# A 3x3 convolution by small tiles: shared products written into the columns' accumulators by ScalarE, and four products in five of six row combinations

## The chip, the core and the metric

The kernel runs on one core of a Trainium2 chip. Its time is the device time of one execution in microseconds (us). A core has five engines that run side by side and wait for one another through semaphores: TensorE (PE; its weight loads are listed as PEld) multiplies matrices into PSUM, an accumulator memory of eight banks; VectorE (DVE) and ScalarE (ACT) work element by element and can read and write PSUM and SBUF; GpSimd (POOL) works element by element on SBUF alone; SyncE (SP) issues DMA transfers. Each engine runs its own instructions in a fixed order.

## The reference

Two residual bottleneck layers, one after the other, in float32, on 64 images of 1024 channels and 14 x 14 pixels:

```python
out = relu(bn(conv(out_of_layer_before, w1, b1, 1, 0), g1, be1))   # 1x1, 1024 -> 256
out = relu(bn(conv(out, w2, b2, 1, 1), g2, be2))                   # 3x3, 256 -> 256
out = bn(conv(out, w3, b3, 1, 0), g3, be3)                         # 1x1, 256 -> 1024
out = relu(x + softplus(residual_scale)[0] * out)
```

`bn` takes the mean and variance of each channel over all images and pixels, so every convolution has to be complete before the next step can use its result.

## The kernel before

**The stages.** For each of the two layers: the first 1x1 convolution (in the first layer alone, in the second fused with the end of the first layer), the 3x3 convolution (`conv2`), a stage that gathers second moments for the last normalization (`gram`, `conv3_stats`), and the last 1x1 convolution with the residual. The 1x1 convolutions use a scheme with seven products for eight (`Seven`). The 3x3 convolution is the stage that the change touches, and two helpers beside it: `filters`, which transforms the 3x3 filters, and `norm`, which applies the normalization.

**How the 3x3 convolution is computed.** The rows of an image are taken four at a time. Six linear combinations of the input rows (i = 0 to 5) are each convolved along the line with a transformed filter, and the six results are combined into four output rows. Along a line, the columns are split into an odd and an even half (`WH` = 7 columns each). For a pair of output columns there are two ways. With *five products* a combination uses D1D2, applied to the sum of the two halves (one product that both columns share), and D1, D3 for the odd and D2, D0 for the even columns. With *four products* it uses SUM and DIFF, applied to the sum and to the difference of the halves (both shared), and D3M1 and D0M2 for one column each; the last two need a further array `v` of column differences. `FOUR` (line 67) lists the combinations with four products: 3, 4 and 5.

**Tiling.** Channels are 2 slots of 128 partitions (`MS`), for input (`s`) and output (`o`). Images go in 8 groups of 8. Combinations 0, 1, 2 and 5 have 4 rows of tiles, so a matmul has 4 x 8 x 7 = 224 columns; 3 and 4 have 3 rows, 168 columns. Each product is 4 matmuls (2 x 2 slots), so a combination is 20 matmuls with five products and 16 with four.

**Per pair of combinations.** `pairs` (line 492) runs over the groups and, in each, over the pairs (1, 2), (3, 4), (5, 0). `combine` makes the row combinations of a pair on VectorE (`r`), and in `ready` the sums of the halves on VectorE (line 531), the differences on GpSimd (line 534), `v` on VectorE (line 538) with its edges on ScalarE, and starts the load of the transformed filters `u` (line 547). `products` runs the matmuls of the pair. `finish` evacuates: ScalarE copies one shared product to SBUF (`ms`, lines 657 and 661); VectorE forms the half with the shared parts (`shared_part`, line 675) and adds the columns' own products (`column`, line 683). Then VectorE combines the results into output rows, which overwrite the input rows in `y`. The loop makes the combinations of the next pair before the products of the present one. For group 0 and the last group VectorE takes statistics (`stat`, line 693), for the others ScalarE does (`moment`, line 755).

**Order and buffers.** A scheduler of the language orders the instructions of each engine, except where the kernel fixes the order (`keep_in_program_order`). In `conv2` TensorE's matmuls are not fixed. All eight PSUM banks rotate under one tag, `ps`: a combination takes three or four in turn. Line 63 gives the numbers of SBUF buffers.

**Filters.** `filters` makes the transformed filters. For the first layer it runs on VectorE beside the first convolution. For the second layer it runs on GpSimd beside the moments stage (line 1101), in four pieces, with scratch tiles (`spare`) from the pool that holds the x tiles; the x tiles of the next stage (line 1121) reuse these buffers.

Of the kernel before, what the change touches and what calls it, by code (L numbers as in the profile page):

```python
# [33 lines left out]
FP = mybir.dt.float32  # L35
# [3 lines left out]
P = 128  # L39
# [23 lines left out]
BUFS = dict(u=3, t=3, r=4, sums=4, diffs=2, v=2, ms=3, f=2)  # L63
# [3 lines left out]
FOUR = 3, 4, 5  # L67
NKS = [4 if i in FOUR else 5 for i in range(NF)]
NK = max(NKS)
D0, D1D2, D3, D1, D2 = range(5)  # L70
D0M2, SUM, DIFF, D3M1 = range(4)
# [11 lines left out]
def bottlenecks(ctx: ExitStack, tc: tile.TileContext, x, w1s, w2s, w3s, pars, out):  # L83
# [73 lines left out]
    def filters(eng, b, s, o, spare):  # L157
# [24 lines left out]
        for i, (row, more, op, by) in parts.items():  # L182
# [7 lines left out]
            if i in FOUR:  # L190
                r0, r1, r2 = (row[:, k * P : (k + 1) * P] for k in range(3))
                ends = rest[:, w : w + P]
                eng.tensor_tensor(ends, r0, r2, ALU.add)
                eng.tensor_tensor(u[:, SUM], ends, r1, ALU.add)
                eng.tensor_tensor(u[:, DIFF], ends, r1, ALU.subtract)
                scaled(u[:, SUM : DIFF + 1], u[:, SUM : DIFF + 1], 0.5 * by)
                scaled(u[:, D0M2], r0, -by)
                scaled(u[:, D3M1], r2, by)
            else:
                scaled(u[:, 0:3, :].rearrange("p k m -> p (k m)"), row, by)  # L200
                eng.tensor_tensor(
                    u[:, D1 : D2 + 1], u[:, D0 : D3 + 1 : D3 - D0], u[:, D1D2 : D1D2 + 1].to_broadcast([P, 2, P]),
                    ALU.subtract,
                )
# [275 lines left out]
    def norm(s, y, aff):  # L480

        scale, shift = aff
        nc.scalar.activation(y, y, AF.Relu, bias=shift[:, s : s + 1], scale=scale[:, s : s + 1])
# [6 lines left out]
    def conv2(psum, pool, b, par, aff, stats):  # L490

        pairs = [(g, p) for g in range(NG) for p in ((1, 2), (3, 4), (NF - 1, 0))]
# [23 lines left out]
        def combine(g, pair, between=None):  # L516
# [4 lines left out]
            made = []  # L521

            def ready(i, r):
# [21 lines left out]
                u = pool.tile([P, MS * MS * NK * P], FP, tag="u", name="u", bufs=BUFS["u"])  # L545
                u = u[:, : MS * MS * NKS[i] * P].rearrange("p (s o k m) -> p s o k m", s=MS, o=MS, m=P)
                nc.sync.dma_start(out=u, in_=us[b][i])
                made.append((i, lines, r, sums, diffs, u))

            both = slice(0, MS)  # L550
            if pair[0] == 1:
# [11 lines left out]
                ready(1, ra)  # L563
                nc.vector.tensor_sub(rb, t1, t2)
                ready(2, rb)
            elif pair[0] == 3:
# [6 lines left out]
                ready(3, ra)  # L573
                stt(rb, t4, -2.0, t3)
                ready(4, rb)
            else:
# [7 lines left out]
                ready(NF - 1, rb)  # L584
                for s in range(MS):
                    stt(ra[:, s, 1:], rows(g, s, 0, 1, RT), 4.0, ra[:, s, 1:])
                ready(0, ra)
            return made

        def products(made, first):  # L590


            done = []
            for i, lines, r, sums, diffs, u in made:
                n = lines * WH
                four = i in FOUR

                def bank():
                    return psum.tile(2 * RT * GI * WH).rearrange("p (o n) -> p o n", o=MS)

                less = bank() if four else None
                m = bank()
                eos = [bank() for o in range(MS)]

                def shared(to, k, v, o, s):
                    nc.tensor.matmul(  # L606
                        to[:, o, :n], u[:, s, o, k], v[:, s].rearrange("p l c -> p (l c)"),
                        start=(s == 0), stop=(s == MS - 1),
                    )

                def columns(o, s, part):

                    odd, even = (eos[o][:, q, :n].rearrange("p (l c) -> p l c", c=WH) for q in range(2))
                    if four:
                        to, k, v = ((odd, D3M1, r[:, s, :, WH:]), (even, D0M2, r[:, s, :, :WH]))[part]
                        nc.tensor.matmul(to, u[:, s, o, k], v, start=(s == 0), stop=(s == MS - 1))  # L616
                        return
                    to, k, v = (
                        (odd, D1, r[:, s, :, WH:]),
                        (odd[:, :, : WH - 1], D3, r[:, s, :, WH + 1 :]),  # L620
                        (even, D2, r[:, s, :, :WH]),
                        (even[:, :, 1:], D0, r[:, s, :, : WH - 1]),
                    )[part]
                    start = s == 0 and part % 2 == 0
                    stop = s == MS - 1 and part % 2 == 1
                    if by_slot:

                        start, stop = s + part == 0, s == MS - 1 and part == 3
                    nc.tensor.matmul(to, u[:, s, o, k], v, start=start, stop=stop, skip_group_check=by_slot)  # L629

                by_slot = first and not done
                each = list(itertools.product(range(MS), range(MS)))
                if four:
                    for to, k, v in ((less, DIFF, diffs), (m, SUM, sums)):
                        for o, s in each:
                            shared(to, k, v, o, s)
                    for o in range(MS):
                        for part in range(2):
                            for s in range(MS):
                                columns(o, s, part)  # L640
                elif by_slot:
                    for s, o in each:
                        for part in range(4):
                            columns(o, s, part)
                    for o, s in each:
                        shared(m, D1D2, sums, o, s)
                else:
                    for o in range(MS):
                        for s in range(MS):
                            shared(m, D1D2, sums, o, s)  # L650
                        for part in range(4):
                            for s in range(MS):
                                columns(o, s, part)
                ms = pool.tile([P, MS, RT * GI * WH], FP, tag="ms", name="ms", bufs=BUFS["ms"])
                if i == 1:
                    for o in range(MS):
                        nc.scalar.activation(
                            ms[:, o, :n], m[:, o, :n], AF.Identity, bias=par[:, B2 + o : B2 + o + 1]
                        )
                else:  # L660
                    nc.scalar.activation(ms[:, :, :n], (less if four else m)[:, :, :n], AF.Copy)  # L661
                done.append((four, lines, m, ms, eos))
            return done

        def halves(f, lines):

            return f.rearrange("p o r (i q c) -> p o q (r i) c", i=GI, q=2)[:, :, :, :lines]

        def shared_part(item, f):

            four, lines, m, ms, eos = item
            if four:
                a, l = (v[:, :, : lines * WH].rearrange("p o (l c) -> p o l c", c=WH) for v in (m, ms))
                for q, op in enumerate((ALU.subtract, ALU.add)):
                    nc.vector.tensor_tensor(halves(f, lines)[:, :, q], a, l, op)

        def column(item, f, o):
            four, lines, m, ms, eos = item
            n = lines * WH
            to = more = halves(f, lines)[:, o]  # L680
            if not four:
                more = ms[:, o, None, :n].to_broadcast([P, 2, n]).rearrange("p q (l c) -> p q l c", c=WH)
            nc.vector.tensor_tensor(to, eos[o][:, :, :n].rearrange("p q (l c) -> p q l c", c=WH), more, ALU.add)

        def finish(g, pair, done, acc):

            fa, fb = (new("f", full if pair[0] == 3 else RT) for i in range(2))
            out_rows = [y_grp[:, :, g, k::4, :] for k in range(4)]
            to = {0: first_stats, NG - 1: stats[:, :, 1:]}.get(g)

            def stat(o, k, lines):
                if to is not None:
                    nc.vector.bn_stats(to[:, o, k, :], lines[:, o])

            if pair[0] in (1, 3):
                for item, f in zip(done, (fa, fb)):
                    shared_part(item, f)
                    for o in range(MS):
                        column(item, f, o)
            if pair[0] == 1:  # L700
                acc = new("fa"), new("fb")
                nc.vector.tensor_add(acc[0], fa, fb)
                nc.vector.tensor_sub(acc[1], fa, fb)
            elif pair[0] == 3:
                a, d = (v[:, :, :full] for v in acc)
                c, e = (new(tag, full) for tag in ("fc", "fd"))
                nc.vector.tensor_add(c, fa, fb)
                nc.vector.tensor_sub(e, fa, fb)
                for o in range(MS):
# [7 lines left out]
            else:  # L717
# [9 lines left out]
                for o in range(MS):  # L727
                    stat(o, 4, end)
# [441 lines left out]
```

## Time and profile before

Three runs: 2070.30, 2070.74 and 2072.93 us; the median is 2070.74. The profiled execution has a span of 2069.7 us at a granted TensorE clock of 0.987.

| engine | busy, us | share of the span |
|---|---|---|
| TensorE, matmuls | 2009.1 | 97% |
| TensorE, weight loads | 1709.2 | 83% |
| VectorE | 1572.0 | 76% |
| ScalarE | 809.3 | 39% |
| GpSimd | 657.5 | 32% |

The 3x3 convolution of the first layer lies between about 312 and 621 us, that of the second between about 1341 and 1647. The profile shows busy time for each engine, for the whole span or for a stretch of it, the chain of work that ended last, groups of equal instructions with their mean time and what they waited for, and the instructions in order of time. A line of the order of time gives start and length in us, the engine, the source line, the operation, what it writes and reads, and in brackets how long the engine was idle before it and what ended the idle time. A float32 matmul of the program shows as two records. Matmuls are pipelined, so the distance between two starts tells more of their cost than the length of one.

### The profile page before, as it was taken

How to read it: one execution, taken by the hardware profiler on the slowest of the kernel's cores; microseconds unless marked ns; L12 is line 12 of the kernel's file. 1: busy time of each engine (PE TensorE's matmuls, PEld its weight loads, DVE VectorE, ACT ScalarE, POOL GpSimd, SP SyncE). 2: the span in 40 equal slices, each digit the busy share in tenths (PEclk: the TensorE clock that was granted, in tenths of full speed). 3: DMA queues.
4: the chain of work that ended last, by engine and by line, in shares of the span. 5: the costliest groups of instructions: out<-in, count | busy, mean ns of one | idle time of the engine just before them, and what ended most of it. 6: DMA issues, size and time to landing. Idle time of an engine off the chain costs nothing.

```text
span 2069.7 us, 27894 instructions
## 1 busy us (share of the span) xinstructions
PE 2009.1 (97%) x10120; PEld 1709.2 (83%) x10120; DVE 1572.0 (76%) x2946; ACT 809.3 (39%) x1591; POOL 657.5 (32%) x668
## 2 busy tenths in 40 slices
PE   8999998999998989999999999899999899999998
PEld 4555558999998879999999999899999898555554
DVE  6776559999883466777777767699989734799997
ACT  1011116224225035555555555462332330555555
POOL 0100001122218953333343333210322000566665
PEclk9999999999999989999999999999999999999999
DMA  7664425555533244444444444255555420589998
GB/s 285 235 240 162 184 94 191 181 206 184 199 138 125 99 190 160 183 168 176 183 160 187 160 184 172 100 197 197 194 181 206 160 92 20 222 320 339 326 340 300
DMA packets 73338, 395.33 MB, mean 191 GB/s; under 512 B 7024, under 2 KB 38000, under 8 KB 44400
## 3 DMA queue, kind: packets, MB, share of 16 engines
q1 hardware_dynamic: 63168, 324.26, 43.6%
q10 hardware_dynamic: 5904, 51.91, 6.0%
q0 software_dynamic: 4128, 17.37, 2.2%
q8 instruction: 80, 1.31, 0.3%
q14 instruction: 58, 0.48, 0.1%
HBM read 276.60 MB, written 116.92 MB: 190 GB/s over the span
## 4 chain that ended last, share of the span: by engine, by line
PE 80%; DVE 6%; POOL 6%; DMA 4%; issue 3%; ACT 1%; SPq 0%; DVEq 0%; POOLq 0%; ACTq 0%
PE ay L155 13%; PE ps L629 13%; PE cy L155 13%; PE ps L606 9%; PE ap L155 7%; PE cp L155 7%; PE ps L616 6%; PE ax L155 4%; PE cx L155 4%; POOL spare L168 2%; PE cp L810 2%; DMA x<-mid 2%; DVE x L400 2%; PE ps L155 1%; PE ap L811 1%
## 5 line engine op out<-in xcount | busy, mean ns | idle before, releaser
L274 ACT ACTIVATE cu<-cy,scale 128x196 f32<-128x196 f32 (+1 forms) x552 | 257.0, 474 | 305.8 <-PE cy L155 297.4
L534 POOL TENSOR_TENSOR diffs<-r 128x336 f32<-128x336 f32 (+1 forms) x48 | 115.5, 2408 | 651.3 <-DVE r L514 453.9
L629 PE MATMUL ps<-r,u 128*128 128x224 f32 (+1 forms) x1536 | 293.7, 343 | 13.9 <-DVE r L562 7.0
L629 PEld LDWEIGHTS ps<-r,u 128*128 128x128 f32 x1536 | 279.3, 190 | 17.8 <-issue 14.8
L400 DVE SCALAR_TENSOR_TENSOR x<-cp,scale,x 128x196 f32<-128x196 f32 (+1 forms) x368 | 178.0, 484 | 84.4 <-PE cp L155 82.3
L274 ACT ACTIVATE x<-x,shift 128x392 f32<-128x392 f32 x368 | 211.7, 614 | 68.4 <-POOL x L426 52.1
L155 PE MATMUL cy<-ct,w3s 128*128 128x196 f32 (+1 forms) x736 | 222.3, 384 | 2.5 <-ACT cu L274 2.5
L421 POOL TENSOR_TENSOR x<-x,cu 128x196 f32<-128x196 f32 (+1 forms) x184 | 167.7, 912 | 175.6 <-ACT cu L274 167.8
L155 PE MATMUL ay<-at,w1s 128*128 128x196 f32 (+1 forms) x752 | 209.3, 381 | 1.0 <-ACT au L274 1.0
L426 POOL TENSOR_TENSOR x<-x,cu 128x392 f32<-128x392 f32 x124 | 125.9, 1015 | 193.3 <-DVE x L400 188.5
L155 PEld LDWEIGHTS ay<-at,w1s 128*128 128x128 f32 x752 | 136.5, 190 | 35.4 <-ACT au L274 1.9
L155 PEld LDWEIGHTS cy<-ct,w3s 128*128 128x128 f32 x736 | 134.2, 191 | 36.8 <-ACT cu L274 4.0
L606 PE MATMUL ps<-sums,u 128*128 128x224 f32 (+1 forms) x768 | 156.0, 337 | 0.0
L447 POOL TENSOR_TENSOR x<-x,cu 128x392 f32<-128x392 f32 x120 | 125.1, 1042 | 83.4 <-DVE x L400 78.4
L274 ACT ACTIVATE au<-ay 128x196 f32<-128x196 f32 (+1 forms) x141 | 53.7, 381 | 241.7 <-PE ay L155 235.8
L661 ACT ACTIVATE ms<-ps 128x448 f32<-128x448 f32 (+1 forms) x80 | 40.4, 504 | 266.8 <-PE ps L606 266.8
L606 PEld LDWEIGHTS ps<-sums,u 128*128 128x128 f32 x768 | 133.0, 189 | 0.1
L400 DVE SCALAR_TENSOR_TENSOR x<-cx,scale,x 128x196 f32<-128x196 f32 (+1 forms) x184 | 89.1, 484 | 57.0 <-PE cx L155 51.3
L155 PE MATMUL cy<-y,w 128*128 128x196 f32 (+1 forms) x416 | 130.4, 401 | 1.1 <-DVE x L891 1.1
L616 PE MATMUL ps<-v,u 128*128 128x168 f32 (+1 forms) x768 | 131.1, 322 | 0.0
L155 PE MATMUL cx<-y,w 128*128 128x196 f32 (+1 forms) x404 | 125.9, 397 | 0.6 <-DVE x L891 0.6
L616 PEld LDWEIGHTS ps<-v,u 128*128 128x128 f32 x768 | 123.8, 188 | 0.8
(209 smaller groups left out, 4080.3 us busy)
## 6 DMA issues: line engine op xcount, KB each, us to landing
x<-in_x SPq DMA_DIRECT2D x62, 1568.0 KB, 6.6
u<-u SPq DMA_DIRECT2D x48, 1280.0 KB, 5.5
x<-mid SPq DMA_DIRECT2D x32, 1568.0 KB, 9.3
u<-u SPq DMA_DIRECT2D x48, 1024.0 KB, 4.8
mid<-x ACTq DMA_DIRECT2D x31, 1568.0 KB, 5.1
out<-x SPq DMA_DIRECT2D x124, 392.0 KB, 6.6
u<-y POOLq DMA_DIRECT2D x12, 320.0 KB, 5.7
u<-spare POOLq DMA_DIRECT2D x12, 320.0 KB, 2.5
```

The lines of the kernel that those rows point to most:

```text
L155: tc.keep_in_program_order(nc.tensor.matmul(*args, **kw))
L168: eng.tensor_scalar(to, v, by, None, ALU.mult)
L274: tc.keep_in_program_order(nc.scalar.activation(*args, **kw))
L400: nc.vector.scalar_tensor_tensor(v, bank, self.scale[:, o : o + 1], v, ALU.mult, ALU.add)
L421: nc.gpsimd.tensor_add(self.part(1, 1), self.part(1, 1), u3)
L426: nc.gpsimd.tensor_add(v, v, self.u12)
L447: nc.gpsimd.tensor_add(v, v, self.u12[:, i * self.n : (i + 1) * self.n])
L534: nc.gpsimd.tensor_sub(diffs, r[:, :, :, :WH], r[:, :, :, WH:])
L606: nc.tensor.matmul(to[:, o, :n], u[:, s, o, k], v[:, s].rearrange("p l c -> p (l c)"), start=(s == 0), stop=(s == MS - 1),)
L616: nc.tensor.matmul(to, u[:, s, o, k], v, start=(s == 0), stop=(s == MS - 1))
L629: nc.tensor.matmul(to, u[:, s, o, k], v, start=start, stop=stop, skip_group_check=by_slot)
L810: nc.tensor.matmul(g0, zt[:, c, 0:P], zt[:, c, :], start=first, stop=last)
```

## The change

**Four products in more combinations.** `FOUR` becomes 0, 2, 3, 4, 5; only combination 1 keeps five products. This saves four matmuls each for combinations 0 and 2. `filters` makes the four-product filters for these two as well.

**Shared products go into the columns' banks.** A combination now has one bank for both output slots of its odd columns and one for the even columns. TensorE first runs the product that goes to both (DIFF with four products, D1D2 with five) into a bank of its own, `l` or `m`. ScalarE copies it, for DIFF with the sign of the half, into the odd and the even bank. TensorE then accumulates the columns' own products on top (`start=False`). With four products the SUM product still goes to SBUF (`ms`), and VectorE adds it while it evacuates (`add`). With five products nothing is left to add, and VectorE reads the two banks when it joins combination 1 with combination 2 into `fa` and `fb`. Four matmuls with the identity open the column banks once per layer.

**The order.** Work goes by single combinations, in the order 1, 2, 3, 4, 5, 0, in three steps: `start` (the first shared product and ScalarE's writes), `middle` (SUM and `ms`) and `columns`. TensorE's order is now fixed: start of the next combination, then middle and columns of the present one. The banks have four tags with two buffers each (`l`, `m`, `odd`, `even`). Norms and moments on ScalarE are spread over the combinations (`long_work`) and kept in order. The load of `u` is split into `ua` (the first shared filter) and `ub` (the rest).

```diff
-BUFS = dict(u=3, t=3, r=4, sums=4, diffs=2, v=2, ms=3, f=2)
+BUFS = dict(ua=4, ub=3, t=2, r=4, sums=4, diffs=3, v=3, ms=3, f=2)
-FOUR = 3, 4, 5
+FOUR = 0, 2, 3, 4, 5
...
+        for tag in COLUMNS * 2:
+            n = MS * RT * GI * WH
+            matmul(psum.tile(n, tag), ident, ident[:, :1].to_broadcast([P, n]), start=True, stop=True)
...
+            def start(self):
+                if self.first:
+                    self.columns()
+                    return
+                v = self.whole("l", DIFF, self.diffs) if self.four else self.whole("m", D1D2, self.sums)
+                self.banks = [self.bank(tag) for tag in COLUMNS]
+                if self.four:
+                    for bank, sign in zip(self.banks, (-1.0, 1.0)):
+                        nc.scalar.activation(bank, v, AF.Copy, scale=sign)
                 else:
+                    self.biased(self.banks, v)
+            def middle(self):
+                self.ms = None
+                if self.four or self.first:
+                    m = self.whole("m", SUM if self.four else D1D2, self.sums)
...
+                    self.biased([self.ms], m)
...
+            def add(self, f):
+                for q in range(2):
+                    nc.vector.tensor_tensor(
+                        half(f, q), self.column(q), self.column(q, self.ms), ALU.add
+                    )
...
+                fa = None if ca.ms is None else outputs(ca)
+                fb = outputs((yield))
+                a, d = new("fa"), new("fb")
+                if fa is not None:
+                    nc.vector.tensor_add(a, fa, fb)
+                    nc.vector.tensor_sub(d, fa, fb)
+                else:
+                    for q in range(2):
+                        nc.vector.tensor_tensor(half(a, q), ca.column(q), half(fb, q), ALU.add)
+                        nc.vector.tensor_tensor(half(d, q), ca.column(q), half(fb, q), ALU.subtract)
...
+        for k in range(NG * NF):
+            queue.extend(itertools.islice(made, 1))
+            for item in queue[1:2]:
+                item.start()
+            item = queue.pop(0)
+            item.middle()
+            if not item.first:
+                item.columns()
+            finished.send(item)
+            long_work(*divmod(k, NF))
...
-            conv2(Psum(scope, ["ps"], ps=8), pool, b, pb, aff, stats2)
+            conv2(Psum(scope, ["l"], l=2, m=2, odd=2, even=2), pool, b, pb, aff, stats2)
```

## The prediction

> **What bounds the kernel now.** I read the page first: TensorE is busy for 97% of the span and holds 80% of the chain that ended last. Then I went to the stage that changes, the 3x3 convolution, with a table of busy time over two stretches of 37 us, each one image group long, and over the stage behind it.
>
> ```profile
> core 0: us, PE busy (x) PEld busy (x) DVE busy (x) ACT busy (x) POOL busy (x), PEclk, DMA share, GB/s
> 421.00:458.00 37.00, 37.00 (x218) 36.78 (x217) 35.34 (x64) 12.12 (x25) 9.08 (x3) 1.00 0.55 192
> 458.00:495.00 37.00, 37.00 (x218) 36.78 (x217) 34.33 (x61) 12.11 (x25) 9.08 (x3) 1.00 0.54 192
> 640.00:740.00 100.00, 96.72 (x603) 84.15 (x603) 50.66 (x91) 13.39 (x14) 95.39 (x135) 0.98 0.25 91
> ```
>
> In the convolution TensorE never pauses, but VectorE has only 2.7 us of every 37 left. In 640 to 740 us GpSimd is busy for 95 of 100 us: it transforms the second layer's filters. The order of time shows what that leads to:
>
> ```profile
> 743.83 0.60 POOL L205 DMA_DIRECT2D u<-spare  x1 [0.30 <-POOL spare L168]
> 743.20 9.14 SPq L118 DMA_DIRECT2D x<-in_x  x3
> 751.41 0.42 DVE L400 SCALAR_TENSOR_TENSOR x<-cx,scale,x 128x196 f32<-128x196 f32 x1 [5.59 <-DMA x<-in_x]
> 752.22 1.02 PE L155 MATMUL cp<-y,w3s 128*128 128x196 f32 x2 [6.01 <-DVE x L400]
> ```
>
> The x tiles that the next stage needs reuse the filters' scratch tiles. Their load starts when GpSimd ends, and TensorE stands still for 6.01 us. So GpSimd's filter chain, 629 to 744 us, lies on the path today.
>
> TensorE's own pieces, from its order of time in one group:
>
> ```profile
> 457.68 1.67 PE L606 MATMUL ps<-diffs,u 128*128 128x224 f32 x8
> 463.77 0.92 PE L606 MATMUL ps<-sums,u 128*128 128x224 f32 x4
> 470.99 0.92 PE L606 MATMUL ps<-sums,u 128*128 128x224 f32 x4
> 485.45 1.30 PE L606 MATMUL ps<-diffs,u 128*128 128x168 f32 x8
> 490.05 1.30 PE L606 MATMUL ps<-diffs,u 128*128 128x168 f32 x8
> ```
>
> Starts apart: combination 5 (four products, 16 matmuls of 224 columns) takes 6.09 us, a five-product combination (20 matmuls) 7.22, combinations 3 and 4 (16 of 168 columns) 4.60 each. A group is 6.09 + 3 x 7.22 + 2 x 4.60 = 36.95 us; combination 5 starts 36.97 us apart from group to group.
>
> GpSimd beside VectorE, both in the convolution:
>
> ```profile
> 460.22 5.39 POOL L534 TENSOR_TENSOR diffs<-r 128x336 f32<-128x336 f32 x1 [8.89 <-DVE r L514]
> 464.75 1.14 DVE L675 TENSOR_TENSOR f<-ps,ms 128x448 f32<-128x448 f32 x2
> 398.19 0.93 POOL L534 TENSOR_TENSOR diffs<-r 128x336 f32<-128x336 f32 x1 [19.67 <-DVE r L514]
> 487.19 2.06 DVE L702 TENSOR_TENSOR fa<-f 128x896 f32<-128x896 f32 x1
> ```
>
> The same difference of 336 elements takes 0.93 us or 5.39. In the second case it ends only once VectorE reaches an operation that reads PSUM (464.75). The other way round, the addition of 896 elements takes 2.06 us beside a GpSimd difference instead of the usual 1.08.
>
> **What the Trainium skill says.** "SBUF — State Buffer", section "Who interferes with whom": a VectorE instruction with two SBUF inputs contends with a GpSimd instruction that reads SBUF, and one of them blocks fully. The lines above agree (5.39 against 0.93 us; 2.06 against 1.08). "PSUM — Partial Sum Buffer", "The four PSUM rules": writes of ScalarE leave a bank's written-bits alone, and a matmul without the start flag adds where they are set. That is why the change opens every column bank once with an identity matmul; no run here shows it yet. "ScalarE: Activation LUTs", "What ACT_TABLE_LOAD costs": an activation with immediates takes 186 ns + 0.833 ns per element, 559 ns for 448; the trace has 543 (L661).
>
> **The change part by part.** *TensorE.* Combinations 0 and 2 go from five products to four: 2 x (7.22 - 6.09) = 2.26 us less per group. TensorE alone would take 34.7. Over 16 groups that is the 36 us that the change is for. The four identity matmuls per layer (448 columns, about 0.75 us each by 392 columns in 0.66) fall into the 7 us for which TensorE waits at the start of the stage; I price them at nothing.
>
> *ScalarE.* Bank writes are 6 of 448, 4 of 336 and 4 of 224 elements per group, at 0.54, 0.45 and 0.43 us. With the moments and norms that it has already, it stays under 25 us of 37, so it is no bound, though it runs in order.
>
> *VectorE.* I count the built kernel's instructions for one group and price them by the distance between starts back to back: 0.53 us for 448 elements, 0.42 for 336, 0.77 for 672, 1.00 for 896, 0.86 for 768, 0.67 for 576, 0.30 for 224. Before: 16, 28, 8, 4, 1, 2, 1, which is 32.9 us. After: 14, 22, 9, 3, 3, 2, 1, which is 30.8. Before really took 34.33, so contention with three GpSimd operations costs 1.4. After has five such operations (differences for 0 and 2 too): 1.4 x 5/3 = 2.3, at least 1.4. VectorE needs about 33 us.
>
> *The new wait, and the one that I think decides.* Each kind of column bank has two buffers, taken in turn by combinations 1, 2, 3, 4, 5, 0. Combination 1's banks are read only together with the finished result of 2 (fa and fb), and 3 needs the same banks next. So ScalarE cannot write 3's even bank, and TensorE cannot run 3's even columns, before VectorE is through; behind them in TensorE's fixed order stand the first products of 5 and all of 4, and VectorE's next step waits for 4. One turn of this loop: VectorE from its read of 4's odd bank to the last reader of 1's even bank in the next group is all its work but four instructions (three of 336, one of 768), 30.8 - 2.1 = 28.7, plus 0.3 of waiting for 4's even bank; ScalarE 0.45 and two hand-overs of 0.1; TensorE 1.15 (even columns of 3) + 1.52 (first products of 5) + 1.15 + 1.15 (sums and odd columns of 4) = 4.97. Sum 34.6, plus contention of 1.4 to 2.3: 36.0 to 36.9. I take 2.3, since the two added GpSimd operations run beside the same stream of two-input additions, and call it 37.0: the same pace as today. Seven periods in each of two layers: 0.
>
> *Group 0.* Its statistics are VectorE work inside that loop: bn_stats and aggregates take about 4.3 us (1.73 for four, 0.91 for two, 0.44 for two, 0.6 twice, 0.28 twice). Today eight rotating banks let TensorE run on; the loop cannot. +4.3 per layer. Start and end differ by about +1: the first products of 5 come some 1 us earlier in group 0, since part of 4 now stands behind them, and that part comes back at the end. Together 2 x 5.4 = 10.8.
>
> *Filters of the second layer, on GpSimd.* A five-product filter costs a scaling of 384 and a subtraction of 256: 1.17 + 0.73 = 1.90 us. A four-product one costs 0.46 + 0.52 + 0.53 + 0.85 + 2 x 0.58 = 3.52. Two filters, four pieces: 8 x 1.62 = 13.0, less some 0.05 of overlap for each added instruction: 12. Nothing hides it: TensorE already waits at the end of this chain. +12. The first layer's filters run on VectorE, which is busy 108 of 181 us there: nothing. The loads of u, cut in two, carry fewer bytes and are ordered several combinations ahead: nothing.
>
> Sum: 2070.7 + 0 + 10.8 + 12 = 2093.5, say 2094.
>
> **The rivals.** *TensorE stays the bound (13%).* If GpSimd's operations fall beside VectorE's PSUM reads, contention vanishes and a group takes 34.7: 14 x -2.27 = -32, +2, +12: 2053. For it: VectorE's sum of 30.8 alone fits. Against it: 5.39 us in the lines above. *GpSimd is starved (27%).* The difference for 2 is asked for in a stretch of VectorE work without any PSUM read (from r of 2 to the read of 0's odd bank, 4 us). If it waits as at 460.22, TensorE's first products of 2 wait too: TensorE from these to 4's odd columns 21.4, VectorE from there to the read of 0's odd bank 14.8, GpSimd 1.17, hand-overs 0.2: 37.5 per group, +7 in all: 2101. *Both waits add up (7%).* The difference for 4 is late as well, 38.5 per group: +21 over my forecast, 2115. *The filter chain is hidden (5%).* 2082; it would need TensorE to be later than GpSimd there, against the 6.01 us.
>
> **How the numbers follow.** My forecast has 48%. The range leaves out the first rival and the one of both waits, 20% together: 2068 to 2110; contention at its lower bound (36.0 per group, -13) gives 2081, inside. Faster by over 0.2% is the first rival, 0.13; the space between it and the forecast gives 0.09 for within 0.2%; slower 0.78.
>
> **What would show it.** Right: combination 5 starts about 37 us apart from group to group, TensorE has gaps of 2 us or so per group, at the even columns of 3 or at the first products of 2; GpSimd's filter chain is 12 us longer and TensorE waits about 18 us at its end. Wrong: groups 34.7 us apart with TensorE at 37 of 37 busy, GpSimd differences all near 1 us, or a filter chain that no longer ends last. The weakest number is the contention, 1.4 to 2.3 us.

## The result and the profile after

The changed kernel takes 2106.5 us (median; 2103.7 to 2109.1), the kernel before 2071.8 beside it: 1.0165 times as long, 95% interval 1.0147 to 1.0184. The profiled execution has a span of 2105.4 us, 35.7 more than before. Cut at the same events in both traces (a 3x3 convolution ends here with GpSimd's first instruction after it), these come from:

| stretch | after minus before, us | forecast |
|---|---|---|
| start to the last matmuls of the first layer's first convolution | +2.8 | 0 |
| 3x3 convolution, first layer | +12.2 | +5.4 |
| filters of the second layer, to the load of x | +12.3 | +12 |
| end of the first layer, first convolution of the second | -1.5 | 0 |
| 3x3 convolution, second layer | +10.5 | +5.4 |
| the rest | -0.6 | 0 |

Two of the three large terms are in the 3x3 convolution, so look there first. The table of busy time over one period in the second layer (columns: length, then busy us of TensorE, its weight loads, VectorE, ScalarE, GpSimd, then the clock granted to TensorE):

```profile
1490.08:1527.84 37.76, 35.17 (x200) 34.28 (x201) 33.93 (x55) 21.54 (x43) 10.63 (x5) 1.00 0.52 174
```

Before, TensorE was busy for 37.0 of 37. Now a group takes 37.76 us and TensorE is busy for only 35.2. It has lost the matmuls it was to lose, and the period did not follow. The order of time on TensorE says where the pause is:

```profile
1490.08 1.75 PE L157 MATMUL m<-sums,ua 128*128 128x224 f32 x8 [2.38 <-issue]
...
1496.62 1.78 PE L157 MATMUL l<-diffs,ua 128*128 128x224 f32 x8 [0.21 <-POOL diffs L542]
...
1511.93 1.32 PE L157 MATMUL odd<-v,ub 128*128 128x168 f32 x8
1513.10 1.31 PE L157 MATMUL even<-v,ub 128*128 128x168 f32 x8
...
1516.90 1.32 PE L157 MATMUL odd<-v,ub 128*128 128x168 f32 x8
...
1523.77 1.69 PE L157 MATMUL even<-v,ub 128*128 128x224 f32 x8
1527.84 1.75 PE L157 MATMUL m<-sums,ua 128*128 128x224 f32 x8 [2.38 <-issue]
```

The even columns of combination 3 (1513.10), where the forecast put the wait, follow without a gap. TensorE pauses 2.38 us before `m<-sums,ua`, the first products of combination 1. "issue" means that the profile names no releaser; the operand does. These products read the sums of r for 1, and VectorE's order of time shows when those come:

```profile
1518.32 0.51 DVE L693 TENSOR_TENSOR f<-odd,ms 128x336 f32<-128x336 f32 x1 [2.32 <-ACT ms L636]
...
1525.59 1.08 DVE L578 TENSOR_TENSOR r<-t 128x896 f32<-128x896 f32 x1
1526.59 0.62 DVE L693 TENSOR_TENSOR f<-odd,ms 128x448 f32<-128x448 f32 x1
1527.13 0.61 DVE L539 TENSOR_TENSOR sums<-r 128x448 f32<-128x448 f32 x1
```

VectorE waits for combination 4 (1518.32; the profile names `ms`, which ScalarE had ready at 1517.55, but the odd columns of 4 end last, at 1518.22). Then it does the output arithmetic of the pair (3, 4), with one short wait of 0.34 us, and only then the sums of 1, which end at 1527.74; TensorE starts at 1527.84. That closes a loop: TensorE from the first products of 1 to the odd columns of 4, 1490.08 to 1518.22 = 28.14 us; hand-over 0.10; VectorE from 1518.32 to 1527.74 = 9.42; hand-over 0.10. The sum is 37.76, the period. In the list of waits TensorE stands 18.3 us at this place in each layer. That is about what eight groups were to save, 8 x 2.26 = 18.1.

The chain of filters on GpSimd ends like this now (against 743.20 and 6.01 us before):

```profile
769.52 1.84 POOL L170 TENSOR_SCALAR spare<-spare 128x128 f32<-128x128 f32 x3
770.52 9.07 SPq L120 DMA_DIRECT2D x<-in_x  x3
...
778.33 0.42 DVE L403 SCALAR_TENSOR_TENSOR x<-cx,scale,x 128x196 f32<-128x196 f32 x1 [13.73 <-DMA x<-in_x]
...
779.14 1.02 PE L157 MATMUL cp<-y,w3s 128*128 128x196 f32 x2 [15.04 <-DVE x L403]
```

TensorE waits 15.04 us at its end, 9.0 more than before.

### The profile page after: what moved, and what is told of

The parts are those of the page before. It is cut to its first block, busy times and chain, and to the rows that moved or that the text cites. A ratio compares the mean times of both kernels' runs of the same rounds, so it can differ in the third digit from the quotient of the medians.

```text
span 2105.4 us, 27919 instructions
## 1 busy us (share of the span) xinstructions
PE 1996.8 (95%) x9880; PEld 1682.0 (80%) x9880; DVE 1565.9 (74%) x2892; ACT 909.9 (43%) x1843; POOL 710.7 (34%) x736
## 4 chain that ended last, share of the span: by engine, by line
PE 71%; DVE 10%; POOL 8%; DMA 6%; issue 3%; ACT 1%; SPq 0%; DVEq 0%; POOLq 0%; ACTq 0%
PE ay L157 14%; PE cy L157 12%; PE ap L157 7%; PE cp L157 6%; PE odd L157 5%; PE even L157 5%; PE m L157 5%; PE l L157 5%; PE ax L157 4%; PE cx L157 3%; POOL spare L170 2%; PE cp L864 2%; POOL diffs L542 2%; DMA x<-mid 2%; DVE x L403 2%
## 5 line engine op out<-in xcount | busy, mean ns | idle before, releaser
L542 POOL TENSOR_TENSOR diffs<-r 128x448 f32<-128x448 f32 (+1 forms) x80 | 157.1, 1972 | 623.4 <-DVE r L580 302.7
L157 PE MATMUL cp<-y,w3s 128*128 128x196 f32 (+1 forms) x368 | 114.2, 392 | 17.7 <-DVE x L403 16.3
L157 PE MATMUL m<-sums,ub 128*128 128x224 f32 (+1 forms) x640 | 126.2, 341 | 0.0
L157 PE MATMUL l<-diffs,ua 128*128 128x224 f32 (+1 forms) x640 | 123.0, 335 | 1.9 <-POOL diffs L542 1.9
L864 PE MATMUL cp<-zt 128*128 128x257 f32 x392 | 120.7, 390 | 4.2 <-DVE zt L884 4.2
L157 PE MATMUL odd<-v,ub 128*128 128x224 f32 (+1 forms) x640 | 123.6, 334 | 0.0
L157 PE MATMUL even<-v,ub 128*128 128x224 f32 (+1 forms) x640 | 123.3, 334 | 0.0
L157 PEld LDWEIGHTS m<-sums,ub 128*128 128x128 f32 x640 | 114.5, 196 | 1.0
```

The source lines that it names most:

```text
L157: tc.keep_in_program_order(nc.tensor.matmul(*args, **kw))
L542: nc.gpsimd.tensor_sub(diffs, r[:, :, :, :WH], r[:, :, :, WH:])
L864: nc.tensor.matmul(g0, zt[:, c, 0:P], zt[:, c, :], start=first, stop=last)
```

## The experiments

**The theories.** A: the late sums for combination 1 set the period. B: GpSimd's starved difference for combination 2 does. C: both loops are as good as equally long, and only removing both helps. F: the loop of the forecast, in which combination 3 waits for the banks of 1. For B and C speak these lines of the changed kernel:

```profile
1491.68 4.88 POOL L542 TENSOR_TENSOR diffs<-r 128x448 f32<-128x448 f32 x1 [20.02 <-DVE r L580]
...
1497.42 0.93 POOL L542 TENSOR_TENSOR diffs<-r 128x336 f32<-128x336 f32 x1 [0.86 <-DVE r L524]
```

The difference for 2 takes 4.88 us, another one 0.93, as the rival "GpSimd is starved" had it; it ends at 1496.56, and TensorE starts on it at 1496.62 after waiting 0.21 us.

**Combination 1 started later.** Its first products go behind the columns of 0 in TensorE's order:

```diff
-            for item in queue[1:2]:
-                item.start()
+            ahead = queue[1:2]
+            for item in ahead:
+                if item.i != 1:
+                    item.start()
             item = queue.pop(0)
             item.middle()
             if not item.first:
                 item.columns()
+            for other in ahead:
+                if other.i == 1:
+                    other.start()
```

> The changed kernel, with the first products of combination 1 started only after the columns of combination 0, about 4 us later in TensorE's order; every instruction stays. In the changed kernel a group takes 37.76 us, and TensorE pauses 2.38 us before combination 1, for sums that VectorE makes late. Theory A (the late sums alone set the pace): the pause goes and nothing takes its place at once; a group takes 35 to 36 us, the whole 2072 to 2085. Theory C (two loops are tied: the second runs from TensorE's first products of 2 to the odd columns of 4, 21.6 us, over VectorE to r of 2, 11.1, and over GpSimd's starved difference, 4.9): the pause moves to the first products of 2, a group still takes about 37.5, the whole 2101 to 2107. Theory B (the starved GpSimd alone): as C. Theory F (my forecast, the banks of 1 and 3): no change, 37.76.

Measured: 2076.4 us (ratio to the kernel before 1.0025, 1.0015 to 1.0034), 30 us less than the changed kernel. A group takes 36.22 us, a little more than the 35 to 36 of theory A. The pause before 1 is gone, and one of 1.3 us stands before the products of 2:

```profile
1506.97 1.78 PE L157 MATMUL l<-diffs,ua 128*128 128x224 f32 x8 [1.28 <-POOL diffs L542]
```

So A is right about what bound the kernel, and the whole time lies in its band, but not that nothing takes its place. C is wrong as it was put: its second loop does set the pace now, but a shorter one, because the starved difference shrinks to 3.36 us when the two streams fall against each other differently (21.6 + 11.1 + 3.4 = 36.1):

```profile
1503.55 3.36 POOL L542 TENSOR_TENSOR diffs<-r 128x448 f32<-128x448 f32 x1 [18.48 <-DVE r L580]
```

**The difference for 2 on VectorE.**

```diff
-                    nc.gpsimd.tensor_sub(diffs, r[:, :, :, :WH], r[:, :, :, WH:])
+                    eng = nc.vector if i == 2 else nc.gpsimd
+                    eng.tensor_sub(diffs, r[:, :, :, :WH], r[:, :, :, WH:])
```

> The changed kernel, with the difference for combination 2 alone made by VectorE (about 0.53 us) instead of GpSimd (4.9 us, most of it starved). Theory B (the starved difference sets the pace): a group falls from 37.76 to 35 to 36 us, the whole to 2072 to 2085. Theory A and theory C (the late sums for combination 1 hold TensorE as long as the difference does): the pause of about 2.4 us before combination 1 stays, a group takes 37.2 to 38.2, the whole 2098 to 2112. Theory F (banks): VectorE has 0.5 us more to do in the loop, 38.2 us per group, 2112.

Measured: 2099.1 us (1.0136, 1.0117 to 1.0155), 7 us less than the changed kernel; 37.28 us per group, and the pause stays where it was:

```profile
1525.57 1.68 PE L157 MATMUL l<-diffs,ua 128*128 128x224 f32 x8
...
1556.68 1.75 PE L157 MATMUL m<-sums,ua 128*128 128x224 f32 x8 [2.38 <-issue]
```

B is out: the starvation is real and does not set the pace by itself. The 0.48 us per group that this edit gains are on TensorE: VectorE's part of the loop is 9.42 us as before (1547.16 to 1556.58), TensorE's 27.66 instead of 28.14, and the difference is the wait of 0.21 us in front of the products of 2, which is gone (1525.57). That wait lay inside the loop of A and, from start to start, cost 0.48.

**Both edits.**

> Both edits together: combination 1 starts after the columns of 0, and VectorE makes the difference for 2. Theory C (two tied loops): only now does the group get shorter, to 35 to 36 us, for TensorE's own work is 34.7 and VectorE's about 34.4; the whole 2070 to 2085. Theory A: the same as with the late start alone; theory B: the same as with the difference on VectorE alone. Theory F: no gain, 38 us per group.

Measured: 2065.7 us (0.9973, 0.9966 to 0.9981), 40.8 us less than the changed kernel, 5.5 less than the kernel before, and 4 under the lower end of theory C. One period:

```profile
1464.51:1499.77 35.26, 35.12 (x202) 34.38 (x200) 33.64 (x56) 21.33 (x43) 6.32 (x4) 1.00 0.57 187
```

TensorE is busy for 35.12 of 35.26 us: it is nearly the bound again. The parts alone gave 30 and 7, together 41, so the second edit is worth 11 us once the first is in. Busy time hides a rest: TensorE's own pieces need 34.7 us from start to start, and 0.4 of the other 0.6 lie at the even columns of 3. They start 1.46 us after its odd ones (1481.42), against 1.17 in the changed kernel, and right behind ScalarE's write of their bank, which had waited for VectorE's read of 2's:

```profile
1482.39 0.43 ACT L648 ACTIVATE even<-l 128x336 f32<-128x336 f32 x1 [1.19 <-DVE f L694]
1482.88 1.42 PE L157 MATMUL even<-v,ub 128*128 128x168 f32 x8
```

So a wait for column banks is there after all, milder than the forecast's and for the banks of 2 instead of those of 1. No run here separates what it is worth.

**One filter piece on VectorE.** Of the four pieces of the second layer's filters, the first is made by VectorE beside the moments stage, in two halves:

```diff
                     def piece(s, o):
...
+                        if (s, o) == (0, 0):
+                            return filters(nc.vector, 1, s, o, spare)
                         for _ in filters(nc.gpsimd, 1, s, o, spare):
                             pass
...
+                        beside[2] = lambda: (quarter.append(piece(0, 0)), next(quarter[0]))
+                        beside[8] = lambda: next(quarter[0], None)
```

> The changed kernel, with one of the four pieces of the second layer's filters made by VectorE (in two halves, their stores from SyncE's queue), the other three by GpSimd as before. If GpSimd's filter chain is on the path and costs the 12 us, as the forecast has it: the chain gets about 32 us shorter, the 15.0 us for which TensorE waits at its end shrink to nearly nothing (some wait for the x load remains), and the whole falls by 10 to 16 us, to 2091 to 2097. If the chain was hidden by something else that ends as late (the affine constants or the x load itself): a fall of under 3 us.

Measured: 2094.1 us (1.0109, 1.0092 to 1.0127), 12.4 us less than the changed kernel. The load of x starts at 739.19 instead of 770.52, and the wait of 15 us in front of `cp<-y,w3s` has gone:

```profile
739.19 12.30 SPq L120 DMA_DIRECT2D x<-in_x  x3
...
766.00 0.60 PE L157 MATMUL cp<-y,w3s 128*128 128x196 f32 x2 [0.33 <-DVE x L404]
```

The chain was on the path, as the forecast said. The gain stops near the length of the wait, though the chain ends 31 us earlier.

**The forecast's banks, made real.** In the changed kernel combination 3 gets the banks of 2 (lines in the next section). Here combinations 1, 3, 5 are tied to one pair and 2, 4, 0 to the other:

```diff
-                self.banks = [self.bank(tag) for tag in COLUMNS]
+                self.banks = [self.bank(tag + str((1, 2, 3, 4, 5, 0).index(self.i) % 2)) for tag in COLUMNS]
...
-            conv2(Psum(scope, ["l"], l=2, m=2, odd=2, even=2), pool, b, pb, aff, stats2)
+            conv2(Psum(scope, ["l"], l=2, m=2, odd0=1, odd1=1, even0=1, even1=1), pool, b, pb, aff, stats2)
```

> The changed kernel with the column banks tied to the turn that the forecast assumed: combinations 1, 3, 5 share one pair of banks, 2, 4, 0 the other, each named by hand, so that 3 must wait for the banks of 1. Nothing else is changed. Forecast's theory (banks in turn are what sets the pace): no difference, 37.8 us per group, no gap moves. Theory A (late sums set the pace, and the changed kernel's allocator gives 3 the banks of 2, which come free earlier): a gap appears in TensorE at the even columns of 3; if the forecast's loop is 36 to 37 us, it fits beside the 37.76 and the whole grows by under 5 us; if it is longer than that, by 7 times 2 times the difference.

Measured: 2133.3 us (1.0300, 1.0285 to 1.0315), 27 us more than the changed kernel. A wait now exists where the forecast put it, at the even columns of 3, and the old one is still there:

```profile
1526.39 1.68 ACT L277 ACTIVATE y<-y,shift,scale 128x1568 f32<-128x1568 f32 x1
1527.97 0.44 ACT L647 ACTIVATE even<-l 128x336 f32<-128x336 f32 x1
...
1528.46 1.42 PE L157 MATMUL even<-v,ub 128*128 128x168 f32 x8 [1.30 <-ACT even L647]
1543.32 3.33 PE L157 MATMUL m<-sums,ua 128*128 128x224 f32 x8 [2.38 <-issue]
```

F fell, and so did the "under 5 us" that I gave theory A if the new loop were no longer than the old. The new wait lies inside the old loop, on TensorE between 1 and 4, so the two add up: 37.76 + 1.30, and 39.34 from 1503.98 to 1543.32. Most of this wait is ScalarE's queue and not the bank: VectorE is through with 1's even bank at 1526.58, but ScalarE had begun a normalization at 1526.39 and writes the bank only at 1527.97. (My estimate from these lines: a write at once would have ended near 1527.1, where TensorE was ready for the even columns.)

**The same banks on the kernel with both edits**, where the other two loops are short.

> The same turn of the banks, on the kernel with the late start of combination 1 and the difference for 2 on VectorE, which takes 35.26 us per group. This measures the forecast's loop by itself, since the other two loops are shorter here. If the forecast's sum is right, a group takes 36.0 to 37.0 us with a gap of 1 to 2 us at the even columns of 3, the whole is 2076 to 2092 against 2065.7. If the loop is shorter than TensorE's own work: no gap, 35.3 us per group, 2064 to 2068.

Measured: 2111.1 us (1.0192, 1.0175 to 1.0210). A group takes 38.07 us (39.73 where TensorE's clock drops), more than the band of 36 to 37, and the whole is above 2092 too. The loop piece by piece:

```profile
1509.51 1.42 PE L157 MATMUL even<-v,ub 128*128 128x168 f32 x8 [0.85 <-ACT even L648]
...
1514.84 0.51 DVE L694 TENSOR_TENSOR f<-odd,ms 128x336 f32<-128x336 f32 x1 [2.43 <-ACT ms L637]
...
1545.23 0.61 DVE L729 TENSOR_TENSOR fb<-even,f 128x448 f32<-128x448 f32 x1
```

```profile
1545.49 1.70 ACT L277 ACTIVATE y<-y,shift,scale 128x1568 f32<-128x1568 f32 x1
1547.08 0.45 ACT L648 ACTIVATE even<-l 128x336 f32<-128x336 f32 x1
```

TensorE 5.33 us (1509.51 to 1514.84), VectorE 31.00 (to 1545.84), ScalarE 1.74 (to TensorE's next even columns at 1547.58). VectorE's part is what I forecast: 28.7 + 0.3 + up to 2.3. ScalarE's is not: I priced its write at 0.45 us, and it stands behind a normalization of 1.70 us that began 0.35 us before the bank came free.

**The gains together**: late start, difference for 2, filter piece.

> The late start, the difference for 2 on VectorE, and one of the four filter pieces of the second layer on VectorE, together. If the three act in different places their gains add up: 2106.5 - 40.8 - 12.4 = 2053, between 2050 and 2057. If the filter's gain is taken by a wait that was hidden, it stays above 2060.

Measured: 2054.1 us (0.9919, 0.9904 to 0.9934). The sum of the parts was 2053: the gains add up, so they act in different places.

**The first load of a layer.** TensorE's first columns wait for `ub`, which is loaded behind `ua` (3.69 us in the first layer of the changed kernel, 5.84 in the second). Here the order is turned for the first combination only:

```diff
-                for tag, a, e in (("ua", 0, 1), ("ub", 1, NKS[i])):
+                halves = ("ua", 0, 1), ("ub", 1, NKS[i])
+                begins = g == 0 and i == order[0][0]
+                for tag, a, e in halves[::-1] if begins else halves:
...
+                u = u[::-1] if begins else u
```

> As the one before, and for the very first combination of a layer the larger part of the filters is loaded ahead of the smaller one, since the columns are computed first there. If the wait of 3.7 and 5.8 us for this load at the start of the two convolutions comes from being second in the queue, each shrinks by 0.7 us or more, the whole falls by 1 to 4 us against the kernel without it. If it comes from the transfer alone: no measurable difference.

Measured: 2051.6 us (0.9905, 0.9889 to 0.9922), the fastest kernel of this study, 2.4 us below the one without the turn, with intervals that overlap. The waits fall only from 3.16 to 2.92 us and from 3.42 to 3.14, and what the profile names at their end is now r from VectorE and `ua`. So in the first layer being second in the queue is not what most of the wait was; in the second, where these products do not read `ua`, it stays open. Nor are the 2.4 us shown to be the turn's: in the profiled executions 1.7 of the 3.9 us between them are there before the stage begins (its identity matmuls start at 316.31 instead of 317.97).

**Finer filter portions in the first layer**, three per piece for two.

```diff
-            if i == 2:
+            if i in (1, 3):
                 yield
```

> As the last one (late start, difference for 2 and one filter piece on VectorE, larger part of the filters loaded first), and VectorE makes the first layer's filters in three portions per piece instead of two, so that less of this work stands in one block ahead of the first convolution's outputs. If TensorE's one wait of 5.1 us there (before the products with ap, at 128 us) comes from the size of the portion: it falls to 3 us or less, and the whole by 2 to 5 us, to 2047 to 2050, since TensorE also runs at half pace for a few us after it. If it comes from where the portion falls and not from its size: no measurable difference, 2050 to 2053.

Measured: 2051.9 us (0.9901, 0.9884 to 0.9917), no difference. The last filter now comes so late (251.60 us instead of 137.32) that its scratch lies on outputs of the first convolution's last images and spoils those values; the work done is the same. The wait is where it was:

```profile
128.96 5.59 PE L157 MATMUL ap<-x,w1s 128*128 128x392 f32 x8 [4.97 <-DVE y L329]
```

This does not answer the question. Around the wait VectorE runs the same instructions in nearly the same order as without the edit: the scheduler orders them, and of the 24 filters only the last has moved. So the portions in front of the late output did not get smaller, and whether the wait comes from their size stays open.

## Why the prediction was right, and where it was not

The kernel became slower, as forecast, and 2106.5 us lies inside the range; it lost 35 us where 23 were forecast. Nearly all that is missing is in the two 3x3 convolutions, +22.7 instead of +10.8, and there the reason was not right: that the total comes as near as it does is in part luck (the statistics were priced too high, the longer period and the clock at nothing).

- *TensorE's saving and VectorE's load*: right. From start to start the two pauses cost 2.62 and 0.48 of the 37.76 us, which leaves 34.7 for TensorE, as forecast. VectorE is busy for 33.9 (about 33), ScalarE for 21.5 (under 25). The contention of 1.4 us was read from one stretch of 37 us (34.33); the other one that the prediction shows (35.34) gives 2.4.
- *"The new wait, and the one that I think decides"*: this step failed. It assumed that each kind of bank is "taken in turn by combinations 1, 2, 3, 4, 5, 0", so that "3 needs the same banks next" after 1. The changed kernel gives 3 the banks of 2. ScalarE writes 3's odd bank (1509.05) right after VectorE's one read of 2's (1508.39 and 0.63), while VectorE still has 1's to read:

```profile
1508.39 0.63 DVE L693 TENSOR_TENSOR f<-odd,ms 128x448 f32<-128x448 f32 x1
1509.06 0.63 DVE L727 TENSOR_TENSOR fa<-odd,f 128x448 f32<-128x448 f32 x1
```

```profile
1509.05 0.43 ACT L647 ACTIVATE odd<-l 128x336 f32<-128x336 f32 x1
```

  In the place of this loop stood one that I did not list, over the sums of combination 1. It is shown as the cause: moving the start of 1 removed the pause and took 30 us away. That its 37.76 us is close to my 37.0 is chance. Over the twelve full periods of both layers the 0.79 us between 37.76 and the 36.97 of before make 9.5 us, for which I had 0. The forecast's own step was mis-sized as well: made real, its loop takes 38.07 us, most of the excess being 1.2 us in ScalarE's queue.
- *Group 0's statistics, +4.3 per layer*: too much (and the pieces listed for it add up to 4.8). In each layer the pause behind them is 4.02 us instead of 2.38, so they cost 1.64: of their instructions only the first four stand between 4's odd columns and the sums of 1, and so in the loop:

```profile
1408.51 1.73 DVE L716 BATCH_NORM_STATS2 first_stats<-y 128x6 f32<-128x336 f32 x4
```

```profile
1412.40 3.33 PE L157 MATMUL m<-sums,ua 128*128 128x224 f32 x8 [4.02 <-issue]
```

- *Start of the stage*: the identity matmuls are hidden, as forecast. From the last matmul before to the first column it is 0.8 us longer in the first layer and 2.8 in the second. The load of `ub` ends the wait in both, so the loads of u, put at nothing, do cost something here.
- *Second layer's filters, +12 on the path*: right, +12.3, though TensorE's wait is 15.0 and not 18 us.
- *First layer's filters, nothing*: wrong by 2.8 us. The share that I cited, 108 of 181 us, is of 130 to 311 us; almost all of the filters are made before that (the last is stored at 131.80 us), where VectorE had little room:

```profile
30.00:130.00 100.00, 95.13 (x283) 53.92 (x282) 85.00 (x178) 11.12 (x22) 13.24 (x23) 0.98 0.69 247
```

  In this stage TensorE's waits for VectorE grow from 4.3 to 5.7 us, the longest from 3.95 to 5.22; that is 1.4 of the 2.8.
- *The rival of the starved GpSimd*: the mechanism is there (4.88 us), as "SBUF — State Buffer", section "Who interferes with whom" of the Trainium skill has it for two-input VectorE instructions; most of its time is hidden behind the longer loop; taking it away is worth 7 us with that loop in place and 11 once it is gone.
- A term that I did not have: after some pauses TensorE runs at half clock for a few us. In five of the twelve full periods this adds 1.0 to 2.3 us, 7.9 us in all (see the last section).

## What to carry to other kernels

When an engine is relieved, write down every loop that closes through it, for each operand of each product and each buffer, and not only the one that the change makes new: here one loop of 37.8 us hid a second of 36.2, and a pace of 35.3, close to TensorE's own 34.7, lay behind both. What hands out the buffers decides which loop exists, so read it from the build before pricing one. An instruction that waits in an in-order queue costs what stands ahead of it, and two waits in one loop add up while two in different loops hide each other.

## What the runs showed of the hardware

A pause of TensorE can cost more than its length. A part of this came with every pause looked at: from start to start, the wait listed as 0.21 us cost 0.48, that of 1.30 cost 1.58, that of 2.38 cost 2.62. The larger part came with some. In the changed kernel, after both pauses of 4.02 us and after three of the twelve of 2.38, TensorE fell to half clock (granted clock 0.50 from 401 to 404 us and from 1412.5 to 1417.5). Where this came at once, the same eight matmuls took 3.27 to 3.33 us instead of 1.75. The table of busy time for 4 us after three such pauses of the first layer's convolution in the changed kernel, with the granted clock third from the end:

```profile
400.90:404.90 4.00, 3.98 (x13) 3.71 (x14) 4.00 (x7) 1.16 (x4) 2.38 (x1) 0.61 0.47 171
477.40:481.40 4.00, 3.92 (x21) 3.94 (x22) 4.00 (x7) 2.39 (x8) 2.32 (x1) 1.00 0.64 220
554.10:558.10 4.00, 3.91 (x12) 3.64 (x13) 4.00 (x7) 1.04 (x4) 2.31 (x1) 0.57 0.47 175
```

The clock is 0.57 to 0.61 in two of them and full in the third, and "busy" does not show it: 12 and 13 matmuls instead of 21. The two periods that begin with such a drop take 38.80 and 38.97 us instead of 37.76, and the first period of the second layer, behind a pause of 4.02 us, takes 39.93. With the late start of combination 1, where TensorE's pauses are of 1.3 to 1.5 us, the granted clock is 1.00 over all full periods of both layers (359.48 to 578.66 and 1393.48 to 1612.66). "TensorE: Matmul & The Clock Gate", section "HAM oscillation — how this bites in real kernels", of the Trainium skill warns of idle gaps above about 3.4 us; here gaps of 2.4 us were enough at times.
